# One PSUM bank pair per gate, shared by both halves of a column, in the recurrent layer of a two-layer kernel

## The chip, the cores and the metric

The kernel runs on one core of one Trainium2 chip. The core has TensorE (PE, matrix products), VectorE (DVE), ScalarE (ACT), GpSimd (POOL) and SyncE (SP, which issues DMAs). Each engine takes its own instructions in order, and they wait for each other through semaphores. Matrix products are written to PSUM, here eight banks of 512 fp32 values for each of 128 partitions. The metric is the time of one execution on the device in microseconds (us), lower is better.

## The reference

The input x has shape (4, 64, 256, 256) in fp32. Two layers follow, each added to its input:

```
x = x + L0(groupnorm(x))      # patchwise FFT attention; the change does not touch it
x = x + L1(groupnorm(x))      # below

f = transpose(features, (3, 0, 2, 1))          # columns first: W, B, H, C
def step(prev_col, cur_col):                   # once per column, 255 times
    x = concat([prev one row up, prev, prev one row down])       # 3 x 64 channels
    gi = x @ w_ih.T + b_ih
    gh = cur_col @ w_hh.T + b_hh
    r = sigmoid(i_r + h_r)
    z = sigmoid(i_z + h_z)
    n = tanh(i_n + r * h_n)
    return (1 - z) * n + z * cur_col
```

So layer 1 is a recurrent cell that runs over the 256 columns one after the other. A row of a new column needs three rows of the column before it (itself and its two neighbours).

## The kernel before

**Layer 0** takes the first 4368 us or so. Nothing in it changes.

**Layer 1** (from line 683 to the end of the kernel function) goes through the columns in the loop `for w in range(W)`. The 128 partitions hold two images' 64 channels, and a second index of size 2 (`slot`) the other two, so one instruction works on all four images. A weight is 64 by 64, so a product over all images is four "quarter" matmuls, one for each pair (r, c) of the list `QUARTERS`: r is the half of the partitions that is read, c the half that is written. The four run in different quarters of the array. Each fp32 matmul shows in the trace as two records and two weight loads.

A column's 256 rows are cut in two parts so that one part's matmuls can run while the other's gates are worked out. `parts(w)` gives the cut. It starts at row 144, is one row less in each next column, down to 113, and after 32 columns jumps back to 144. Because it moves by a row a column, part 0 needs only part 0 of the column before. Only where the cut jumps back (columns 33, 65, 97, 129, 161, 193, 225) does part 0 also need part 1 of the column before.

`begin(w, part)` (line 753) does one part; it is called at lines 820 and 821. On PE, in this order, each item being four quarter matmuls:

- h_n (weights `wh[:, 2]` times the column itself) into tile `hr`, index 0
- h_r (`wh[:, 0]`) and three taps of i_r (`wi[:, 0..2]` times the state of the column before, moved by 0, 1 and 2 rows) into `hr`, index 1
- three taps of i_n into tile `nz`, index 0
- h_z and three taps of i_z into `nz`, index 1

Then on ACT and DVE: sigmoid of r (`g`, ACT), a normalisation for a column eight ahead (`xn`, ACT), (h_n + bias) times r (`n`, DVE), plus i_n (`n`, DVE), tanh (`n`, ACT), sigmoid of z (`z`, ACT), and three DVE instructions that end in the new state (`st`). Per column that is ten DVE instructions and eight ACT instructions, part 0's before part 1's on each engine.

The instructions stand on each engine in the order in which the program issues them; the class `InOrder` sees to that. The framework puts in the waits. A PSUM tile of a given tag that is asked for again waits until the last reader of the earlier one is done.

PSUM: the tags are `hr0`, `nz0`, `hr1`, `nz1`, one for each part, and each is two banks, one for each half r. One bank holds two gates side by side (index 0 and 1), 256 values each. That makes 4 x 2 = 8 banks, all there are.

The trace puts every operation on line 156, that of the helper that records the order, so the tiles' names tell the operations apart.

Of the kernel before, what the change touches and what calls it, by code (L numbers as in the profile page):

```python
# [10 lines left out]
F32 = mybir.dt.float32  # L11
AF = mybir.ActivationFunctionType
ALU = mybir.AluOpType
# [3 lines left out]
B, C, W, H = 4, 64, 256, 256  # L17
HID = 6 * C
E = 2 * C
P = 128  # L20
# [141 lines left out]
def tile_conv_then_gru(  # L162
# [17 lines left out]
    nc = InOrder(tc, tc.nc)  # L180
# [25 lines left out]
    wi = const.tile([P, 9, C], F32, tag="wi", name="wi")  # L206
    wh = const.tile([P, 3, C], F32, tag="wh", name="wh")
    for a in range(2):
        at = slice(a * C, (a + 1) * C)
# [3 lines left out]
    bias_sb = const.tile([P, 6], F32, tag="bias", name="bias_sb")  # L213
    nc.scalar.dma_start(bias_sb, bias.rearrange("a o n -> (a o) n"))
    b_rz = const.tile([P, 2], F32, tag="b_rz", name="b_rz")
# [5 lines left out]
    with tc.tile_pool(name="xa", bufs=3) as xa, tc.tile_pool(name="sta", bufs=1) as sta, tc.tile_pool(  # L221
        name="gnps", bufs=1, space=PSUM
# [6 lines left out]
        for kind in range(2):  # L229
            bt = sta.tile([9, NS, HALO], F32, tag="bt", name=f"bt_{kind}")  # L230
            nc.scalar.dma_start(bt, taps[:, kind * NS : (kind + 1) * NS, :])
            for s in range(0, NS, 4):
                to = ts[0:2] if kind == 0 else ts[2:3]
                ps = bps.tile([HALO, 4, len(to) * P], F32, tag="b", name=f"psb_{kind}_{s}")
                for i in range(4):
                    nc.tensor.matmul(
                        ps[:, i, :],
                        lhsT=bt[:, s + i, :],
                        rhs=wd[:, 0 : 2 * P] if kind == 0 else wd[:, 2 * P : 3 * P],
                        start=True,  # L240
                        stop=True,
# [11 lines left out]
        for j in range(NPAIR):  # L253
            st = sta.tile([P, NST, 6], F32, tag="st", name=f"st_{j}", bufs=2)
# [9 lines left out]
        for b in range(B):  # L264
            at = slice((b % 2) * C, (b % 2) * C + C)
# [8 lines left out]
    with ExitStack() as s:  # L274
# [18 lines left out]
        z = big.tile([P, NP, NS], F32, tag="z", name="z")  # L293
# [389 lines left out]
    WB = 8  # L683
    with ExitStack() as s:
        rawp = s.enter_context(tc.tile_pool(name="raw", bufs=3))
        colp = s.enter_context(tc.tile_pool(name="cols", bufs=2))
        gk = s.enter_context(tc.tile_pool(name="gk", bufs=2))
        ps_g = s.enter_context(tc.tile_pool(name="ps_g", bufs=1, space=PSUM))
        raws, xns, xts, stcols = {}, {}, {}, {}

        def columns(m, w):

            yield m[:, :, w, :].rearrange("(k a) c h -> (a c) k h", k=NPAIR), slice(0, P), 0
            for half in range(2):
                b0 = SLOTS[1][0][half]
                yield m[b0 : b0 + 2, :, w + 1, :].rearrange("b c h -> c b h"), slice(half * C, half * C + C), 1

        def load_columns(w):
            n, i = w // WB, w % WB
            if i == 0:  # L700
                raws[n] = rawp.tile([P, 2, WB, H], F32, tag="raw", name=f"raw_{n}")
            for of, at, j in columns(x1, w):
                nc.sync.dma_start(raws[n][at, :, i + j], of)

        def new_columns(n):
            xns[n] = colp.tile([P, 2, WB, H], F32, tag="xn", name=f"xn_{n}")
            xts[n] = colp.tile([P, WB, H], F32, tag="xt", name=f"xt_{n}")

        def empty_states(n):
            stcols[n] = st = colp.tile([P, 2, WB, H + 2], F32, tag="st", name=f"st_{n}")  # L710
            nc.gpsimd.memset(st[:, :, :, 0:1], 0.0)
            nc.gpsimd.memset(st[:, :, :, H + 1 : H + 2], 0.0)

        def normalize(w, slot):
            n, i = w // WB, w % WB
            if i == slot == 0:
                new_columns(n)
            nc.scalar.activation(
                xns[n][:, slot, i],
                raws[n][:, slot, i],  # L720
                AF.Identity,
                bias=sc1[:, w % 2, slot, 0:1],
                scale=sc1[:, w % 2, slot, 1:2],
            )
            if slot and i % 2:

                for half in range(2):
                    nc.sync.dma_start(
                        xts[n][half * C : (half + 1) * C, i - 1 : i + 1],
                        xns[n][(1 - half) * C : (2 - half) * C, half, i - 1 : i + 1],  # L730
                    )

        def add(w):
            n, i = w // WB, w % WB
            nc.gpsimd.tensor_tensor(
                raws[n][:, :, i], raws[n][:, :, i], stcols[n][:, :, i, 1 : H + 1], ALU.add
            )
            if i % 2:
                for of, at, j in columns(out, w - 1):
                    nc.sync.dma_start(of, raws[n][at, :, i - 1 + j])  # L740

        QUARTERS = ((0, 0), (0, 1), (1, 0), (1, 1))
        SKEW = 32

        def parts(w):


            at = H // 2 + SKEW // 2 - (w - 1) % SKEW
            return (0, at), (at, H)

        MAX = H // 2 + SKEW // 2

        def begin(w, part):

            h0, h1 = parts(w)[part]
            i, num = w % WB, h1 - h0
            xn, xt, st = xns[w // WB], xts[w // WB], stcols[w // WB]
            before = stcols[(w - 1) // WB]
            prev = before[:, :, (w - 1) % WB, h0 : h1 + 2]

            cur = {
                (r, c): (xn[:, c] if r == c else xt)[r * C : (r + 1) * C, i, h0:h1] for r, c in QUARTERS
            }
            prevs = [
                {(r, c): prev[r * C : (r + 1) * C, c, t : t + num] for r, c in QUARTERS} for t in range(3)
            ]

            hr = ps_g.tile([P, 2, 2, H], F32, tag=f"hr{part}", name=f"pshr_{w}_{part}")
            nz = ps_g.tile([P, 2, 2, H], F32, tag=f"nz{part}", name=f"psnz_{w}_{part}")

            def quarters(ps, k, weights, rhs, start, stop):
                for r, c in QUARTERS:
                    at = slice(r * C, (r + 1) * C)
                    nc.tensor.matmul(
                        ps[c * C : (c + 1) * C, r, k, 0:num],
                        lhsT=weights[at],
                        rhs=rhs[r, c],
                        start=start,
                        stop=stop,
                        tile_position=(r * C, c * C),  # L780
                    )

            quarters(hr, 0, wh[:, 2, :], cur, True, True)
            quarters(hr, 1, wh[:, 0, :], cur, True, False)
            for t in range(3):
                quarters(hr, 1, wi[:, t, :], prevs[t], False, t == 2)
            for t in range(3):
                quarters(nz, 0, wi[:, 6 + t, :], prevs[t], t == 0, t == 2)
            quarters(nz, 1, wh[:, 1, :], cur, True, False)
            for t in range(3):  # L790
                quarters(nz, 1, wi[:, 3 + t, :], prevs[t], False, t == 2)
            g = gk.tile([P, 2, MAX], F32, tag=f"g{part}", name=f"g_{w}_{part}")[:, :, 0:num]
            n = gk.tile([P, 2, MAX], F32, tag=f"n{part}", name=f"n_{w}_{part}")[:, :, 0:num]
            z = gk.tile([P, 2, MAX], F32, tag=f"z{part}", name=f"z_{w}_{part}")[:, :, 0:num]
            nc.scalar.activation(g, hr[:, :, 1, 0:num], AF.Sigmoid, bias=b_rz[:, 0:1], scale=1.0)
            if w + WB < W:
                normalize(w + WB, part)
            nc.vector.scalar_tensor_tensor(
                n, hr[:, :, 0, 0:num], bias_sb[:, 5:6], g, ALU.add, ALU.mult
            )  # L800
            nc.vector.tensor_tensor(n, nz[:, :, 0, 0:num], n, ALU.add)
            nc.scalar.activation(n, n, AF.Tanh, bias=bias_sb[:, 2:3], scale=1.0)
            nc.scalar.activation(z, nz[:, :, 1, 0:num], AF.Sigmoid, bias=b_rz[:, 1:2], scale=1.0)
            nc.vector.tensor_tensor(g, xn[:, :, i, h0:h1], n, ALU.subtract)
            nc.vector.tensor_tensor(g, g, z, ALU.mult)
            nc.vector.tensor_tensor(st[:, :, i, 1 + h0 : 1 + h1], g, n, ALU.add)

        for w in range(0, 2 * WB, 2):
            load_columns(w)
        for w in range(WB + 1):  # L810
            for slot in range(2):
                normalize(w, slot)
        empty_states(0)
        nc.vector.tensor_copy(stcols[0][:, :, 0, 1 : H + 1], xns[0][:, :, 0])
        for w in range(W):
            n, i = w // WB, w % WB
            if i == 0 and n + 1 < W // WB:
                empty_states(n + 1)
            if w:
                begin(w, 0)  # L820
                begin(w, 1)
            add(w)
            if i % 2 and w + 2 * WB < W:
                load_columns(w + 2 * WB - 1)
# [55 lines left out]
```

## Time and profile before

| | |
|---|---|
| time, median of 3 runs | 5980.89 us (5962.14 to 5995.17) |
| the profiled execution, its own time | 5966.15 us |
| its span, first to last instruction | 5964.4 us |
| mean granted TensorE clock | 0.994 |
| PE busy | 5552.3 us, 93% of the span |
| DVE busy | 4085.5 us, 68% |
| ACT busy | 3438.4 us, 58% |
| POOL busy | 398.9 us, 7% |
| first and last `n` of layer 1 on DVE start at | 4400.6 and 5954.8 us |

Busy time is the time in which at least one instruction of the engine runs. Matmuls are pipelined and the ends of their records are modelled, so a busy PE is not a PE at its limit. "x24" in a line means that so many records follow each other. A form such as 128x284 counts partitions by elements: 284 is a part of 142 rows for both slots. In brackets stands how long the engine was idle before an instruction and what released it; "issue" is idle time in which the engine waited for nothing that the profile shows. Layer 1's matmuls are those that write `pshr` and `psnz`; those that write `psring` are layer 0's.

### The profile page before, as it was taken

The page shows a single profiled execution, that of the slowest core. Times are in us where ns is not written, and L with a number is a line of the kernel's source. Part 1 is how long each engine was busy: PE and PEld are TensorE (multiplying, and loading weights), DVE is VectorE, ACT ScalarE, POOL GpSimd, SP SyncE. Part 2 cuts the span into 40 slices and gives each one's busy share as a digit, 9 for nine tenths or more (in the row PEclk, how much of TensorE's full clock was granted, in tenths as well). Part 3 has the DMA queues.
Part 4 walks back from the last instruction along what each step waited for, and adds up shares of the span by engine and source line. Part 5 has one row for each costly group of instructions (what it writes and reads, how often), then busy time and mean ns, then how long its engine had stood idle before and what let it go on. Part 6 is the DMA issues. An engine that isn't in the chain of part 4 may idle for free.

```text
span 5964.4 us, 282969 instructions
## 1 busy us (share of the span) xinstructions
PE 5552.3 (93%) x129224; PEld 4814.1 (81%) x129224; DVE 4085.5 (68%) x9549; ACT 3438.4 (58%) x4617; POOL 398.9 (7%) x602
## 2 busy tenths in 40 slices
PE   5499999999999999999999999999979999999998
PEld 4388888888887888887888888888868888888888
DVE  7567776666776667677666767667666666666666
ACT  1266656566665656665656666565645555555554
POOL 0000000000000000000000000000002111122121
PEclk9999999999999999999999999999989999999999
DMA  9545454444444444545444544544444444444442
GB/s 386 210 133 151 132 138 143 125 140 145 137 134 138 127 138 142 145 125 146 134 134 131 150 133 131 145 125 141 123 123 111 112 111 110 110 112 113 110 112 80
DMA packets 549714, 818.06 MB, mean 137 GB/s; under 512 B 38443, under 2 KB 432436, under 8 KB 544404
## 3 DMA queue, kind: packets, MB, share of 16 engines
q1 hardware_dynamic: 523264, 683.80, 40.6%
q0 software_dynamic: 22320, 114.70, 5.8%
q8 instruction: 1012, 16.58, 1.2%
q10 hardware_dynamic: 2934, 1.46, 0.1%
q14 instruction: 184, 1.51, 0.1%
HBM read 622.22 MB, written 144.05 MB: 128 GB/s over the span
## 4 chain that ended last, share of the span: by engine, by line
PE 52%; DVE 14%; ACT 6%; issue 4%; DMA 2%; SPq 0%; DVEq 0%; ACTq 0%; POOLq 0%
PE psring L156 45%; DVE g L156 5%; DVE n L156 5%; PE psnz L156 4%; ACT n L156 3%; PE pshr L156 3%; DVE st L156 3%; DMA t<-t_all 2%; ACT v L156 1%; ACT z L156 1%; ACT h L156 0%; DVE z L156 0%; SPq L156 0%; DVEq L156 0%; ACTq L156 0%
## 5 line engine op out<-in xcount | busy, mean ns | idle before, releaser
L156 PEld LDWEIGHTS psring<-h,t 100*32 100x32 f32 x40960 | 1335.6, 115 | 267.1 <-issue 184.3
L156 PE MATMUL psring<-h,t 100*32 100x128 f32 x40960 | 1438.8, 274 | 86.6 <-ACT h L156 35.6
L156 PEld LDWEIGHTS psring<-w_sb,xq 64*100 64x100 f32 x24576 | 1350.2, 163 | 83.0 <-issue 43.6
L156 PE MATMUL psring<-w_sb,xq 64*100 64x128 f32 x24576 | 1391.3, 270 | 25.0 <-POOL xq L156 19.9
L156 ACT COPY h<-psring 100x1024 f32<-100x1024 f32 x1274 | 1203.0, 1027 | 142.4 <-PE psring L156 136.4
L156 PE MATMUL psnz<-st,wi 64*64 64x115 f32 (+16 forms) x24480 | 919.3, 271 | 24.9 <-issue 24.0
L156 PEld LDWEIGHTS psnz<-st,wi 64*64 64x64 f32 x24480 | 778.4, 133 | 46.2 <-issue 45.1
L156 DVE TENSOR_TENSOR pr<-psring,q 128x512 f32<-128x512 f32 (+1 forms) x576 | 464.0, 861 | 339.5 <-PE psring L156 335.8
L156 ACT ACTIVATE n<-n,bias_sb 128x288 f32<-128x288 f32 (+7 forms) x510 | 259.8, 509 | 665.0 <-DVE n L156 665.0
L156 DVE BATCH_NORM_STATS2 lnst<-z 128x6 f32<-128x64 f32 x4096 | 545.2, 214 | 118.2 <-ACT z L156 118.2
L156 DVE TENSOR_TENSOR z<-z,lnm 128x1024 f32<-128x1024 f32 x512 | 612.7, 1218 | 8.7
L156 ACT COPY q<-psring 128x1024 f32<-128x1024 f32 x256 | 259.1, 1012 | 522.4 <-PE psring L156 456.9
L156 PE MATMUL pshr<-st,wi 64*64 64x144 f32 (+7 forms) x12240 | 478.1, 275 | 79.2 <-DVE st L156 63.9
L156 ACT COPY z<-psring 128x2048 f32<-128x2048 f32 x128 | 238.8, 1866 | 499.3 <-PE psring L156 499.3
L156 PE MATMUL psring<-pr,g_sb 32*64 32x512 f32 x8192 | 488.7, 599 | 8.3 <-issue 8.3
L156 ACT ACTIVATE y<-psring,ln_sb 128x512 f32<-128x512 f32 x512 | 372.1, 781 | 200.8 <-PE psring L156 196.9
L156 PEld LDWEIGHTS pshr<-st,wi 64*64 64x64 f32 x12240 | 363.8, 133 | 149.3 <-DVE st L156 93.7
L156 DVE COPY h<-psring 100x1024 f32<-100x1024 f32 x262 | 320.4, 1223 | 217.5 <-PE psring L156 215.3
L156 DVE TENSOR_TENSOR g<-xn,n 128x288 f32<-128x288 f32 (+7 forms) x510 | 217.4, 426 | 325.2 <-ACT n L156 325.2
L156 DVE TENSOR_TENSOR y<-psring,y 128x1024 f32<-128x1024 f32 x256 | 312.3, 1220 | 118.3 <-ACT y L156 116.8
L156 POOL TENSOR_TENSOR raw<-raw,st 128x512 f32<-128x512 f32 x256 | 303.4, 1185 | 1234.0 <-DVE st L156 652.2
L156 PE MATMUL pshr<-xn,wh 64*64 64x144 f32 (+7 forms) x4080 | 354.4, 270 | 9.6 <-ACT xn L156 6.5
(88 smaller groups left out, 6368.5 us busy)
## 6 DMA issues: line engine op xcount, KB each, us to landing
t<-t_all SPq DMA_DIRECT2D x768, 400.0 KB
xq<-in_xh POOLq DMA_DIRECT2D x128, 800.0 KB, 4.6
xc<-in_x SPq DMA_DIRECT2D x32, 2048.0 KB
xr<-in_x SPq DMA_DIRECT2D x256, 256.0 KB
x<-xr SPq DMA_DIRECT2D x256, 256.0 KB
raw<-x SPq DMA_DIRECT2D x128, 256.0 KB
raw<-x SPq DMA_DIRECT2D x256, 128.0 KB
xt<-xn SPq DMA_DIRECT2D x256, 128.0 KB
```

The costliest lines, as they stand in the source:

```text
L156: return self.tc.keep_in_program_order(got(*args, **kwargs))
```

## The change

`begin` becomes `column(w)`, which issues the matmuls of both parts, and `state(w, part, ...)`, which issues a part's ACT and DVE work. Each gate now has a bank pair of its own (tags `hn`, `hr`, `ni`, `hz`, again 4 x 2 = 8 banks), and for `hr`, `ni` and `hz` the two parts take it in turn. h_n is computed once a column over all 256 rows, one matmul per quarter, before everything else of the column; the parts read their rows of it. The arithmetic is the same, and ACT's and DVE's instructions stand in the same order. The order of PE's work in a column is now h_n; h_r and i_r, i_n, h_z and i_z of part 0; the same of part 1. That is 92 matmuls a column where there were 96.

```diff
-        def begin(w, part):
+        def bank_pair(gate, w):
+            return ps_g.tile([P, 2, 512], F32, tag=gate, name=f"ps{gate}_{w}")
+
+        def quarters(ps, weights, rhs, start, stop):
+            for r, c in QUARTERS:
+                nc.tensor.matmul(
+                    ps[c * C : (c + 1) * C, r],
+                    lhsT=weights[r * C : (r + 1) * C],
+                    rhs=rhs(r, c),
...
+        def column(w):
+
+            i, xn, xt, st = w % WB, xns[w // WB], xts[w // WB], stcols[(w - 1) // WB]
+
+            def own(ps, gate, h0, h1, stop):
...
+            def taps(ps, gate, h0, h1, start):
+                for t in range(3):
...
+            pn = bank_pair("hn", w)[:, :, 0:H]
+            own(pn, 2, 0, H, True)
+            for part in range(2):
+                h0, h1 = parts(w)[part]
+                pr, pi, pz = (bank_pair(gate, f"{w}_{part}")[:, :, 0 : h1 - h0] for gate in ("hr", "ni", "hz"))
+                own(pr, 0, h0, h1, False)
+                taps(pr, 0, h0, h1, False)
+                taps(pi, 2, h0, h1, True)
+                own(pz, 1, h0, h1, False)
+                taps(pz, 1, h0, h1, False)
+                state(w, part, pn[:, :, h0:h1], pr, pi, pz)
+
+        def state(w, part, pn, pr, pi, pz):
...
-            hr = ps_g.tile([P, 2, 2, H], F32, tag=f"hr{part}", name=f"pshr_{w}_{part}")
-            nz = ps_g.tile([P, 2, 2, H], F32, tag=f"nz{part}", name=f"psnz_{w}_{part}")
...
-            quarters(hr, 0, wh[:, 2, :], cur, True, True)
-            quarters(hr, 1, wh[:, 0, :], cur, True, False)
-            for t in range(3):
-                quarters(hr, 1, wi[:, t, :], prevs[t], False, t == 2)
-            for t in range(3):
-                quarters(nz, 0, wi[:, 6 + t, :], prevs[t], t == 0, t == 2)
-            quarters(nz, 1, wh[:, 1, :], cur, True, False)
-            for t in range(3):
-                quarters(nz, 1, wi[:, 3 + t, :], prevs[t], False, t == 2)
...
-            nc.scalar.activation(g, hr[:, :, 1, 0:num], AF.Sigmoid, bias=b_rz[:, 0:1], scale=1.0)
+            nc.scalar.activation(g, pr, AF.Sigmoid, bias=b_rz[:, 0:1], scale=1.0)
...
-            nc.vector.scalar_tensor_tensor(
-                n, hr[:, :, 0, 0:num], bias_sb[:, 5:6], g, ALU.add, ALU.mult
-            )
-            nc.vector.tensor_tensor(n, nz[:, :, 0, 0:num], n, ALU.add)
+            nc.vector.scalar_tensor_tensor(n, pn, bias_sb[:, 5:6], g, ALU.add, ALU.mult)
+            nc.vector.tensor_tensor(n, pi, n, ALU.add)
...
-            nc.scalar.activation(z, nz[:, :, 1, 0:num], AF.Sigmoid, bias=b_rz[:, 1:2], scale=1.0)
+            nc.scalar.activation(z, pz, AF.Sigmoid, bias=b_rz[:, 1:2], scale=1.0)
...
             if w:
-                begin(w, 0)
-                begin(w, 1)
+                column(w)
```

More of the change, by code (lines that the diff above doesn't have):

```diff
@@ L751, in tile_conv_then_gru @@
         MAX = H // 2 + SKEW // 2
-        def begin(w, part):
+        def bank_pair(gate, w):
[6 more added lines that the diff above has]
+                    rhs=rhs(r, c),
+                    start=start,
+                    stop=stop,
+                    tile_position=(r * C, c * C),
+                )
@@ new lines, in column @@
+        def column(w):
+            i, xn, xt, st = w % WB, xns[w // WB], xts[w // WB], stcols[(w - 1) // WB]
+            def own(ps, gate, h0, h1, stop):
+                quarters(
+                    ps,
+                    wh[:, gate, :],
+                    lambda r, c: (xn[:, c] if r == c else xt)[r * C : (r + 1) * C, i, h0:h1],
+                    True,
+                    stop,
+                )
+            def taps(ps, gate, h0, h1, start):
+                for t in range(3):
+                    quarters(
+                        ps,
+                        wi[:, 3 * gate + t, :],
+                        lambda r, c: st[r * C : (r + 1) * C, c, (w - 1) % WB, h0 + t : h1 + t],
+                        start and t == 0,
+                        t == 2,
+                    )
+            pn = bank_pair("hn", w)[:, :, 0:H]
[9 more added lines that the diff above has]
+                state(w, part, pn[:, :, h0:h1], pr, pi, pz)
@@ L755, in begin @@
+        def state(w, part, pn, pr, pi, pz):
             h0, h1 = parts(w)[part]
             i, num = w % WB, h1 - h0
[L757 to L766, printed above, removed]
@@ L768, in begin @@
-            hr = ps_g.tile([P, 2, 2, H], F32, tag=f"hr{part}", name=f"pshr_{w}_{part}")
-            nz = ps_g.tile([P, 2, 2, H], F32, tag=f"nz{part}", name=f"psnz_{w}_{part}")
[L771 to L780, printed above, removed]
-                    )
@@ L783, in begin @@
-            quarters(hr, 0, wh[:, 2, :], cur, True, True)
-            quarters(hr, 1, wh[:, 0, :], cur, True, False)
-            for t in range(3):
-                quarters(hr, 1, wi[:, t, :], prevs[t], False, t == 2)
-            for t in range(3):
-                quarters(nz, 0, wi[:, 6 + t, :], prevs[t], t == 0, t == 2)
-            quarters(nz, 1, wh[:, 1, :], cur, True, False)
-            for t in range(3):
-                quarters(nz, 1, wi[:, 3 + t, :], prevs[t], False, t == 2)
+            xn, st = xns[w // WB], stcols[w // WB]
@@ L794, in begin @@
             z = gk.tile([P, 2, MAX], F32, tag=f"z{part}", name=f"z_{w}_{part}")[:, :, 0:num]
-            nc.scalar.activation(g, hr[:, :, 1, 0:num], AF.Sigmoid, bias=b_rz[:, 0:1], scale=1.0)
+            nc.scalar.activation(g, pr, AF.Sigmoid, bias=b_rz[:, 0:1], scale=1.0)
             if w + WB < W:
                 normalize(w + WB, part)
-            nc.vector.scalar_tensor_tensor(
-                n, hr[:, :, 0, 0:num], bias_sb[:, 5:6], g, ALU.add, ALU.mult
-            )
-            nc.vector.tensor_tensor(n, nz[:, :, 0, 0:num], n, ALU.add)
+            nc.vector.scalar_tensor_tensor(n, pn, bias_sb[:, 5:6], g, ALU.add, ALU.mult)
+            nc.vector.tensor_tensor(n, pi, n, ALU.add)
             nc.scalar.activation(n, n, AF.Tanh, bias=bias_sb[:, 2:3], scale=1.0)
-            nc.scalar.activation(z, nz[:, :, 1, 0:num], AF.Sigmoid, bias=b_rz[:, 1:2], scale=1.0)
+            nc.scalar.activation(z, pz, AF.Sigmoid, bias=b_rz[:, 1:2], scale=1.0)
             nc.vector.tensor_tensor(g, xn[:, :, i, h0:h1], n, ALU.subtract)
```

## The prediction

> **What bounds the kernel now.** The page's chain of waits gives most of the span to TensorE in the first layer ("PE psring L156 45%"), which the change doesn't touch. So I left the page and read layer 1 alone, from about 4400 us to the end. First the busy time by stretch (columns: stretch, its length, then busy us and count for PE, weight loads, DVE, ACT, POOL; then clock, DMA share, GB/s):
>
> ```profile
> 5200.00:5400.00 200.00, 184.66 (x6316) 172.52 (x6312) 137.86 (x329) 112.95 (x263) 39.70 (x41) 1.00 0.41 112
> ```
>
> PE looks full (92%) and DVE not (69%). The timeline of DVE says otherwise. One column, in order (start, length, instruction, idle time before it and its releaser):
>
> ```profile
> 5199.99 0.51 DVE L156 SCALAR_TENSOR_TENSOR n<-pshr,bias_sb,g 128x284 f32<-128x284 f32 x1
> 5200.60 0.46 DVE L156 TENSOR_TENSOR n<-psnz,n 128x284 f32<-128x284 f32 x1
> 5201.71 0.46 DVE L156 TENSOR_TENSOR g<-xn,n 128x284 f32<-128x284 f32 x1 [0.66 <-ACT n L156]
> ...
> 5203.14 0.45 DVE L156 SCALAR_TENSOR_TENSOR n<-pshr,bias_sb,g 128x228 f32<-128x228 f32 x1
> ...
> 5205.95 0.51 DVE L156 SCALAR_TENSOR_TENSOR n<-pshr,bias_sb,g 128x282 f32<-128x282 f32 x1
> ```
>
> From one column's first DVE instruction to the next column's: 5.96 us. In it DVE runs ten instructions back to back and stops twice, each time for its own tanh on ACT (0.66 and 0.61 us). It never waits for PE. The chain of waits over 5190 to 5230 confirms it:
>
> ```profile
> by line: DVE g L156 29.6%; DVE n L156 27.2%; ACT n L156 15.6%; DVE st L156 14.9%; issue 9.6%; DVEq L156 1.4%; ACT z L156 1.1%; ACT g L156 1.0%; ACTq L156 0.6%
> ```
>
> No PE in it. PE waits for the state instead, 0.48 us in this column. The DVE list is the same before and after the change, so 5.96 us a column is a floor that the change can't move. Waits of layer 1 (total us, times, longest):
>
> ```profile
> DVE g L156 <- ACT n L156: 324.5, 509, 0.9
> ...
> PE pshr L156 <- DVE st L156: 63.9, 136, 3.0
> ...
> DVE n L156 <- ACT g L156: 33.6, 8, 20.5
> ...
> DVE n L156 <- PE psnz L156: 24.0, 47, 2.3
> ```
>
> The last two rows are what PE costs DVE: 20.5 of the 33.6 is the start of the layer, the rest the seven columns where the boundary jumps back; 24.0 is DVE waiting for the bank of n and z.
>
> **How much lies above the floor.** By the tile answers, n's first DVE instruction starts at 4400.6 and the last (part 1 of column 255) at 5954.8. Less 3.15 for part 0 to part 1 in a column, 254 columns took 1551.0 us. 254 x 5.96 is 1513.8. So 37.2 us are above the floor, in three kinds.
>
> *Boundary columns* (seven: part 0 needs part 1 of the column before). An undisturbed one:
>
> ```profile
> 5769.74 0.97 PE L156 MATMUL pshr<-st,wi 64*64 64x144 f32 x24 [2.96 <-DVE st L156]
> 5770.50 0.94 PE L156 MATMUL psnz<-st,wi 64*64 64x144 f32 x24
> ...
> 5771.30 0.52 DVE L156 SCALAR_TENSOR_TENSOR n<-pshr,bias_sb,g 128x288 f32<-128x288 f32 x1 [1.71 <-ACT g L156]
> ...
> 5771.48 0.94 PE L156 MATMUL psnz<-st,wi 64*64 64x144 f32 x24
> ...
> 5772.48 0.46 DVE L156 TENSOR_TENSOR n<-psnz,n 128x288 f32<-128x288 f32 x1 [0.66 <-PE psnz L156]
> ```
>
> The addition of i_n starts at 5772.48, just after the z matmuls end (5771.48 + 0.94 = 5772.42), although the i_n matmuls end a microsecond earlier: n and z share a bank pair. Two columns take 14.34 us here (5763.48 to 5777.82), 2.42 over the floor; seven times, 16.9 us.
>
> *Half clock.* In four of the seven, PE's clock record shows 0.5 for 3.4 us after the long idle stretch, and the same matmuls take nearly twice as long (1.68 where it was 0.94):
>
> ```profile
> 4790.99 0.99 PE L156 MATMUL pshr<-st,wi 64*64 64x144 f32 x24 [2.96 <-DVE st L156]
> 4791.75 1.68 PE L156 MATMUL psnz<-st,wi 64*64 64x144 f32 x24
> ```
>
> These four cost 6.4 us more (three by 1.66, one by 1.43).
>
> *Hiccups*, the other 13.9 us. PE stops for "issue" every 128 matmul records:
>
> ```profile
> 4621.38 0.47 PE L156 MATMUL psnz<-st,wi 64*64 64x140 f32 x8 [0.46 <-issue]
> ...
> 4625.40 0.70 PE L156 MATMUL pshr<-st,wi 64*64 64x139 f32 x16 [0.36 <-issue]
> ...
> 4629.42 0.43 PE L156 MATMUL psnz<-st,wi 64*64 64x117 f32 x8 [0.25 <-issue]
> ```
>
> They are 4.02 us apart. The DMA view counts 382 instruction packets (6.26 MB, 16 KB each) for PE's 382 blocks of 256 instructions (a matmul record and its weight load each count one).
>
> **What the Trainium skill says.** "PSUM — Partial Sum Buffer", section "PSUM bank collisions raise a hardware error", tells to guard by bank, not by address: two engines may not touch one bank and quadrant at once. That is why the addition waits for z (0.66 us above; agrees). "TensorE: Matmul & The Clock Gate", Part 1: a window of about 3.4 us with too little PE work halves the clock; the four half-clock stretches agree. "Runtime: NRT & Kernel Launch", section "Instruction fetch mechanics": refill in 16 KiB blocks of 256 instructions, "mostly hidden"; the block size agrees, the hiding fails here.
>
> **The change part by part.** One group of four quarter matmuls (eight records) costs 1.70 ns a column of its width: 24 records of 141 columns take 0.72 us (5204.05 to 5204.77).
>
> 1. *h_n in one matmul per quarter.* Same streamed width, 256 instead of 144 + 112, so no PE time; four matmuls fewer a column: 16 of 384 PE instructions, 4.2%. The width 256 isn't in the trace before; from the rate, 256 x 1.70 = 0.44 us. The nearest wider row (8192 records of 512 columns, 488.7 us busy, eight to a round) gives 0.48 for 512 in one pass, so 0.24 for 256 and 0.48 for the two passes. I take 0.44; bounds 0.40 to 0.88 (no overlap of quarters).
>
> 2. *i_n in a bank of its own.* In the boundary columns the addition no longer waits for z. i_n ends at 5771.23 + 0.24; the product before it ends at 5771.82; the addition starts at 5771.92, 0.56 earlier. Seven times: **-3.9 us**. Elsewhere the wait was hidden already: nothing.
>
> 3. *One bank pair per gate for both parts: new waits.* Part 1's r waits for part 0's sigmoid, its i_n for part 0's addition, its z for part 0's z sigmoid. In the column above, PE would come to part 1's r after the sigmoid of part 0 (4.90 + 0.49 = 5205.39), to i_n about 0.5 us after the addition ends (5207.02), to z about when the sigmoid ends; each is due on ACT or DVE only later. Nothing.
>
> 4. *h_n waits for part 1 of the column before.* This is the wait that matters: one h_n pair, freed by part 1's first DVE instruction, and behind it on PE, which takes matmuls in order, stands all of the next column. DVE frees it at 5203.14 + 0.45 = 5203.59 and wants the next sigmoid for 5205.95: 2.36 us. The way through: hand-over 0.06 (state end to matmul, above), h_n 0.44, r's own 0.24, taps 0.72, end of the last 0.245 (0.97 less 0.72), 0.06, sigmoid 0.49, 0.03: 2.28. Margin 0.08. With part 0 at 143: 2.33 against 2.29, margin 0.04. With part 0 at 113 (5760.84 to 5763.48): 2.64 against 2.04, margin 0.60. So it just fits: nothing, but the cover is thin, 0.32 on average, where r had over a microsecond.
>
> 5. *Half clock.* In a boundary column h_n now can't start before 5766.86 + 0.06, so PE's idle 2.96 us splits into about 0.6 before h_n and 2.1 after r's own. The shorter stretches should halve the clock about twice in place of four times: **-3 us** (0 to -6).
>
> 6. *Hiccups.* At 4.02 us a block, 384 instructions take 6.03 us a column, over the floor; 368 take 5.78, under it. Most should be hidden; those that hit h_n or r (22% of the stream) have less cover than before. I take half of the 13.9: **-8 us** rounded, bounds +5 to -13.
>
> No DMA, ACT or POOL instruction moves. Sum: -3.9 - 3 - 8 = **-15 us**. The profiled execution took 5966.15 us (span 5964.4 and 1.75 around it), so 5951; the median shown, 5980.89, is 14.7 above it, so **5966** on that scale. A measurement here tells no change from about 0.5%, 30 us: this forecast is "within".
>
> **Rivals.**
> - *Nothing comes of it* (0 us, 5981): hiccups now strike the thin chain of step 4 and give back what steps 2 and 5 bring. For it: 0.04 of margin at the start of each 32 columns. Against: fewer instructions.
> - *All of it comes* (5942): all removable excess goes, 37.2 less 7 x 1.86 that the boundary needs, 24 us, and the 15 us by which the median exceeds the profiled run were hiccups of layer 1 too. Against: the first layer, 70% of the time and full of PE, can hold those 15.
> - *Slower, the h_n bank is the new loop* (6021): if h_n with its hand-over costs 0.5 us more than I say (quarters that hardly overlap), step 4's chain passes DVE's wherever the margin is less. Margins are spread evenly from 0.04 to 0.60, so the mean loss is 0.46 squared / (2 x 0.56) = 0.19 us on 247 columns, 47 us, less 7 from steps 2 and 5: +40. It decides from about 0.1 us, and passes 0.5% near 0.45. Against: 512-wide matmuls overlap well in the first layer.
>
> **Numbers.** Forecast 58%, nothing 20%, all 13%, slower 9%. Forecast's own range 5948 to 5985. Taking in half of the outer cases and the spread of the runs (5962 to 5995): 5940 to 5992. Faster by over 0.5%: 0.17 (all of it, and a little of the forecast); slower 0.09; within 0.74.
>
> **What would show it.** Right: DVE's column still 5.96 us; boundary columns some 0.56 shorter, the row "DVE n <- PE" nearly gone; PE waiting at pshn for DVE n in most columns, 0.5 to 0.9 us; fewer "issue" stops. Wrong: "DVE n <- ACT g" in ordinary columns (step 4 lost), above all just after a boundary column; or a DVE column below 5.96, which would mean that I misread the floor.

## The result and the profile after

The changed kernel takes 5958.19 us in the median (5941.98 to 5977.76, 20 runs) against 5979.01 us before, 20.8 us less. The ratio is 0.9966 with a 95% interval of 0.9957 to 0.9976: a gain of a third of a percent, clear of noise. The forecast was 5966 us and "within 0.5%". On a second chip the ratio came out as 0.9912 (0.9894 to 0.9929), a gain of 49.7 us; see experiment 6.

In the profiled executions the span goes from 5964.4 to 5950.2 us, 14.2 less. "Layer 1" below means the time from the first column's first DVE instruction to the last column's: 1551.3 us before, 1533.7 after, 17.6 less. The part ahead of it, where nothing was changed, took 3.5 us longer this time.

DVE's waits in layer 1 after the change (total us, times, longest):

```profile
DVE g L156 <- ACT n L156: 325.2, 510, 1.0
DVE n L156 <- ACT g L156: 34.2, 8, 21.2
...
DVE n L156 <- PE pshz L156: 0.9, 2, 0.5
DVE n L156 <- PE psni L156: 0.8, 2, 0.4
```

The two tanh waits of each column are where they were. The row with PE's `psnz`, 24.0 us in 47 waits before, has shrunk to 1.7 us in four.

A boundary column in the timeline after (start, length, engine, instruction, idle before it):

```profile
4789.08 0.97 PE L156 MATMUL pshr<-st,wi 64*64 64x144 f32 x24 [1.92 <-DVE st L156]
4789.84 0.94 PE L156 MATMUL psni<-st,wi 64*64 64x144 f32 x24
4790.64 0.52 DVE L156 SCALAR_TENSOR_TENSOR n<-pshn,bias_sb,g 128x288 f32<-128x288 f32 x1 [1.71 <-ACT g L156]
4790.82 0.94 PE L156 MATMUL pshz<-st,wi 64*64 64x144 f32 x24
4791.26 0.46 DVE L156 TENSOR_TENSOR n<-psni,n 128x288 f32<-128x288 f32 x1
```

The addition starts at 4791.26 while the z matmuls still run to 4791.76. Before, it waited for their end. The pair of columns around an undisturbed jump takes 13.78 us in place of 14.34 (7.82 + 5.96 against 7.82 + 6.52).

An ordinary column, again from the timeline after:

```profile
5203.96 0.45 DVE L156 SCALAR_TENSOR_TENSOR n<-pshn,bias_sb,g 128x232 f32<-128x232 f32 x1
...
5204.47 0.43 PE L156 MATMUL pshn<-xn,wh 64*64 64x256 f32 x1 [0.49 <-DVE n L156]
...
5205.19 0.89 PE L156 MATMUL pshr<-st,wi 64*64 64x139 f32 x24
...
5206.15 0.49 ACT L156 ACTIVATE g<-pshr,b_rz 128x278 f32<-128x278 f32 x1 [0.30 <-PE pshr L156]
...
5206.79 0.50 DVE L156 SCALAR_TENSOR_TENSOR n<-pshn,bias_sb,g 128x278 f32<-128x278 f32 x1
```

This is the new chain of step 4. Part 1's first DVE instruction ends at 5204.41 and frees the h_n bank, PE starts h_n at 5204.47, and the sigmoid that hangs on it ends at 5206.64. DVE, which comes round for it at 5206.79, is not held up, by 0.15 us. The chain of waits over 5210 to 5250 shows how close the two chains have come. Before there was no PE in it:

```profile
by line: DVE n L156 24.3%; DVE g L156 21.8%; ACT n L156 14.3%; DVE st L156 10.7%; issue 9.2%; PE pshr L156 6.8%; PE pshz L156 4.4%; PE psni L156 3.9%; PE pshn L156 2.7%; ACT g L156 1.2%; DVEq L156 1.2%; ACTq L156 0.5%
```

Where the 17.6 us went, from the start times of the columns, always over a floor of 5.957 us a column: the 14 columns around the seven jumps lie 15.6 us over the floor (23.4 before), the other 240, called ordinary below, 5.0 us (14.9 before). PE stops for issue are down from 107 to 29 in these two executions, and the half-clock stretches from four to two. A stop is counted here and below when it is over 0.06 us; the waits view lists those over 0.15 us.

### The profile page after: what moved, and what is told of

It reads as the page before. It is cut to its first block, busy times and chain, and to the rows that moved or that the text cites. A ratio compares the mean times of both kernels' runs of the same rounds, so it can differ in the third digit from the quotient of the medians.

```text
span 5950.2 us, 278865 instructions
## 1 busy us (share of the span) xinstructions
PE 5537.8 (93%) x127184; PEld 4770.7 (80%) x127184; DVE 4085.5 (69%) x9549; ACT 3465.8 (58%) x4617; POOL 399.5 (7%) x602
## 4 chain that ended last, share of the span: by engine, by line
PE 64%; DVE 18%; ACT 7%; DMA 5%; issue 5%; SPq 0%; DVEq 0%; ACTq 0%; POOL 0%; POOLq 0%
PE psring L156 61%; DVE g L156 7%; DVE n L156 6%; DVE st L156 4%; ACT n L156 4%; DMA t<-t_all 2%; DMA xc<-in_x 2%; ACT v L156 2%; ACT z L156 1%; PE pshr L156 1%; PE pshz L156 1%; PE psni L156 1%; ACT h L156 1%; PE pshn L156 0%; SPq L156 0%
## 5 line engine op out<-in xcount | busy, mean ns | idle before, releaser
L156 PE MATMUL psring<-w_sb,xq 64*100 64x128 f32 x24576 | 1394.2, 271 | 27.3 <-POOL xq L156 17.8
L156 PE MATMUL pshr<-st,wi 64*64 64x144 f32 (+7 forms) x12240 | 433.3, 270 | 14.0 <-DVE st L156 13.4
L156 PE MATMUL psni<-st,wi 64*64 64x144 f32 (+7 forms) x12240 | 438.4, 270 | 8.0 <-issue 6.6
L156 PE MATMUL pshz<-st,wi 64*64 64x144 f32 (+7 forms) x12240 | 436.6, 269 | 1.8 <-issue 1.1
L156 PEld LDWEIGHTS psni<-st,wi 64*64 64x64 f32 x12240 | 361.5, 133 | 13.5 <-issue 9.9
```

Of the source, the lines that this page charges most:

```text
L156: return self.tc.keep_in_program_order(got(*args, **kwargs))
```

## The experiments

Two theories of the gain stood against each other. One: PE's stops are rarer because PE has fewer instructions (step 6 of the prediction). The other: the banks do it, because a stop hurts only where DVE waits for PE. Under both lies a claim that is tested first, that DVE with its two tanh waits is the floor.

**1. z without its taps.** In the changed kernel a quarter of PE's work is left out: z is the sigmoid of h_z and the bias alone.

```diff
-                own(pz, 1, h0, h1, False)
-                taps(pz, 1, h0, h1, False)
+                own(pz, 1, h0, h1, True)
```

> The changed kernel without the three taps of i_z (24 of 92 matmuls a column are left out; z is then the sigmoid of h_z and the bias alone). PE has 1.3 us less to do a column. Theory (DVE with its two tanh waits sets 5.96 us a column): layer 1 loses only what is left of PE stops and half clock, so 1526 to 1533 us, time 5950 to 5958. Rival (PE, 92 percent busy, is the bound): 254 x 1.3 us less, about 330 us, time near 5630.

Measured: 5958.82 us, ratio 0.997 (0.996 to 0.9979); layer 1 1534.9 us. Busy time by stretch of this kernel (PE, weight loads, DVE, ACT, POOL, clock, DMA share, GB/s):

```profile
5200.00:5360.00 160.00, 124.85 (x3588) 99.75 (x3592) 110.91 (x264) 93.50 (x212) 31.36 (x32) 1.00 0.41 112
```

PE is down from some 92% to 78%, and the time hasn't moved. PE's work is not what sets the column. The last few us that I expected didn't come either: this trace has no PE stop at all, but half clock at four of the seven jumps. Its ordinary columns still lie 5.7 us over the floor, so the 5.0 us that the changed kernel has left there need no PE stops to explain them.

**2. Two DVE instructions less a column.** The other side of the same question: the last addition is left out of both parts, so the new state is (x - n) times z.

```diff
-            nc.vector.tensor_tensor(g, g, z, ALU.mult)
-            nc.vector.tensor_tensor(st[:, :, i, 1 + h0 : 1 + h1], g, n, ALU.add)
+            nc.vector.tensor_tensor(st[:, :, i, 1 + h0 : 1 + h1], g, z, ALU.mult)
```

> The changed kernel with the last addition left out: the new state is (x - n) times z, so each part has four DVE instructions in place of five. Theory (DVE's list with its tanh waits sets the column): the floor falls by about 0.9 us to 5.04; then PE (5.22 us of matmuls) and the chain of the h_n bank (2.28 + 3.60 - 0.49 = 5.39 at 141 rows, 4.99 at 113) take over, some 5.3 us a column, layer 1 near 1365 us, time 5770 to 5800. Rival (PE is the bound already): at most 10 us off 5958.

Measured on the second chip: ratio 0.9848 (0.9811 to 0.9884), 5911.83 us; layer 1 1479.0 us. The direction is as expected and the size is not: columns at their best take 5.23 to 5.39 us, as worked out, but their mean is 5.82. DVE now waits for the sigmoid of r about once a column, where it did so eight times in the changed kernel, so the chain of the h_n bank has taken over, as expected:

```profile
DVE n L156 <- ACT g L156: 157.5, 265, 20.3
```

What holds this chain back further is in PE's waits:

```profile
PE psni L156 <- issue: 27.9, 46, 1.6
PE pshz L156 <- issue: 24.7, 48, 1.2
PE pshr L156 <- issue: 23.2, 35, 1.8
```

PE stops 163 times for 81 us. The DMA view of layer 1 counts the blocks in which PE's instructions arrive:

```profile
q8 instruction: 364, 5.96, 1.7%
```

Every one of the 163 stops ends between 1.2 and 1.8 us after such a block has landed, with blocks some 4 us apart, so what PE waits for is its instructions. The 95 ordinary columns without a stop take 5.43 us on average, the 145 with one 6.04. That difference goes with the stops. It is not shown to be a fixed rate of the blocks: 364 blocks in 1479 us are one every 4.06 us, and 1.44 blocks a column (368 instructions) times 4.06 give 5.82 us, but that is the mean column over again and no second measurement of it; 28 columns in a row took only 5.68 each.

**3. h_n issued twice.** The margin of step 4, measured by using it up.

```diff
             own(pn, 2, 0, H, True)
+            own(pn, 2, 0, H, True)
```

> The changed kernel with the four h_n matmuls of a column issued twice (the second overwrites the first, same values): +0.44 us of PE behind the wait for part 1's first DVE instruction. Theory (the way from there to the next column's sigmoid has a margin of 0.04 us at part 0 = 143 rows rising to 0.60 at 113): columns of large part 0 take up to 0.40 us more, those below about 121 rows take 5.96 as before, mean 0.14 us, layer 1 +35 us, time 5985 to 6000. Rival (the margin is wide, since PE idles 0.5 us or more before h_n in most columns): within 5 us of 5958. Rival (no margin at all): +0.44 in every column, +110 us.

Measured: 5988.25 us, ratio 1.0022 (1.0011 to 1.0033); layer 1 1566.3 us, 32.6 more than the changed kernel. DVE in the column after a jump now waits for the sigmoid:

```profile
5795.85 0.39 DVE L156 TENSOR_TENSOR st<-g,n 128x224 f32<-128x224 f32 x1
5796.54 0.52 DVE L156 SCALAR_TENSOR_TENSOR n<-pshn,bias_sb,g 128x286 f32<-128x286 f32 x1 [0.30 <-ACT g L156]
```

Row by row, for columns of the last stretch of 32 that nothing else disturbed (margin and excess in us; the margin on a straight line from 0.04 at 143 rows to 0.60 at 113):

| rows of part 0 | margin, predicted | 0.44 less margin | column over 5.957, measured |
|---|---|---|---|
| 143 | 0.04 | 0.40 | 0.37 |
| 134 | 0.21 | 0.23 | 0.21 |
| 131 | 0.26 | 0.18 | 0.15 |
| 128 | 0.32 | 0.12 | 0.09 |
| 125 | 0.38 | 0.06 | 0.05 |
| 122 | 0.43 | 0.01 | 0.00 |

The h_n bank is a chain with just the margin that the trace before gave, some 0.03 us more.

**4. i_n and z in one bank pair again**, all else as changed.

```diff
-                pr, pi, pz = (bank_pair(gate, f"{w}_{part}")[:, :, 0 : h1 - h0] for gate in ("hr", "ni", "hz"))
+                pr = bank_pair("hr", f"{w}_{part}")[:, :, 0 : h1 - h0]
+                nz = ps_g.tile([P, 2, 2, H], F32, tag=f"nz{part}", name=f"psnz_{w}_{part}")
+                pi, pz = (nz[:, :, k, 0 : h1 - h0] for k in range(2))
```

> The changed kernel with i_n and z again side by side in one bank pair per part, h_n and r as changed, order of the matmuls as changed. Theory: only the columns at a jump of the cut notice; in each the addition of i_n waits 0.66 us for the z matmuls again and a pair of columns takes 14.34 in place of 13.78 us, so layer 1 rises by 3.9 us, time about 5962; PE stops for issue as few as after the change. Rival (the own bank of i_n is what hides PE's stops in all columns): many ordinary columns show DVE waiting for PE again, layer 1 rises by 10 us or more, time 5968 or above.

Measured: 6013.99 us, ratio 1.0059 (1.0046 to 1.0072), slower than the kernel before. The theory's 3.9 us came nowhere near. The rival's "10 us or more" takes in the 56 us, but lost cover for PE's stops can't be all of it: the kernel before has the shared bank and the stops too, and is faster. A new theory was worked out for the next trace.

> The same kernel as in the run before with i_n and z in one bank pair, for an undisturbed profile: its time was 6014 us, 56 above the changed kernel, where 3.9 was expected. New theory: with h_n ahead of r in one shared pair the matmuls of part 0 start after part 1's first DVE instruction, about 1 us later than before the change, so the z matmuls of part 0 end after the moment at which DVE wants i_n: by the rates of the trace 0.47 us late at 143 rows, nothing at 113. Columns should grow from 5.96 at small part 0 to about 6.5 at large, layer 1 about 1580 to 1590 us, DVE's waits for PE in the addition some 40 to 55 us in total, nearly all in columns with part 0 above 125 rows. Rival (some other wait, of z or of r): the waits stand elsewhere or in all columns alike.

Measured (one run on the second chip): layer 1 1589.5 us; DVE's row for PE in the addition:

```profile
DVE n L156 <- PE psnz L156: 74.8, 174, 1.9
```

Undisturbed columns lie 0.52 us over the floor at 143 rows, 0.27 at 134, 0.11 at 128 and 0.00 at 122. In the first of these, from DVE's timeline and PE's:

```profile
5838.07 0.51 DVE L156 SCALAR_TENSOR_TENSOR n<-pshn,bias_sb,g 128x286 f32<-128x286 f32 x1
5839.20 0.46 DVE L156 TENSOR_TENSOR n<-psnz,n 128x286 f32<-128x286 f32 x1 [0.62 <-PE psnz L156]
```

```profile
5838.22 0.91 PE L156 MATMUL psnz<-st,wi 64*64 64x143 f32 x24
```

These z matmuls end at 5839.13, and the addition that needs only i_n starts at 5839.20. The new theory holds; the total of the waits, 75 us, is above my 40 to 55, which left out the jumps and PE's stops (44 here). The shared h_n bank makes PE late by about as much as the own bank of i_n lets it be, and without that bank the change makes the kernel slower. The other half alone, an own bank for i_n with h_n as before, was not run. Where i_n and z share a bank pair they are also one tile of the program, in this kernel and in the one before, so whether the wait goes by the bank, as the prediction says, or by the tile stays open.

**5. h_n in two matmuls per quarter again**, 384 PE instructions, new banks.

```diff
-            own(pn, 2, 0, H, True)
+            for h0, h1 in parts(w):
+                own(pn[:, :, h0:h1], 2, h0, h1, True)
```

> The changed kernel with h_n again in two matmuls per quarter (rows of part 0, rows of part 1) into the same shared bank pair, at the same place: 96 matmuls a column, 384 PE instructions, banks as changed. Layer 1 means from the first column's to the last column's first DVE instruction: 1551.3 us before, 1533.7 after. Theory (PE's instruction blocks arrive at about 4.02 us each; 368 instructions a column hide them, 384 do not): the columns at a jump stay 0.56 us shorter than before, but PE stops for issue come back as often as before (about 107 against 29) and layer 1 rises by 6 to 12 us, time about 5966. Rival A (the banks alone made the gain): stops stay near 29 and the time at 5958. Rival B (the thin margin of the h_n chain loses more to such stops than the old order did): slower than before, above 5979.

Measured: 5962.91 us, ratio 0.9974 (0.9965 to 0.9983), which can't be told from the changed kernel's. PE's stops are back, 101 of them for 37 us, but layer 1 takes 1534.9 us, 1.2 more than the changed kernel. Two differences lie in the 1.2: the ordinary columns are 8.5 us over the floor, 3.5 more than the changed kernel's, and the jumps 13.3, 2.3 less, as no jump met half clock in this trace. Nor does the number of PE instructions alone decide how often PE stops: experiment 3's kernel has 384 a column too, and its trace has seven stops.

**6. The old kernel with 92 matmuls.** The converse: old banks, old order, part 1's h_n left out, with the sum for r read in its place.

```diff
-            quarters(hr, 0, wh[:, 2, :], cur, True, True)
+            if part == 0:
+                quarters(hr, 0, wh[:, 2, :], cur, True, True)
...
-                n, hr[:, :, 0, 0:num], bias_sb[:, 5:6], g, ALU.add, ALU.mult
+                n, hr[:, :, part, 0:num], bias_sb[:, 5:6], g, ALU.add, ALU.mult
```

> The kernel before with part 1's h_n matmuls left out (part 1's product reads the sum for r in their place): old banks, old order, but 92 matmuls and 368 PE instructions a column as after the change, and 0.2 us less of PE. Theory (fewer PE instructions hide the arrival of PE's instruction blocks): PE stops for issue fall from 107 to about 30; the columns at a jump still take 14.34 us a pair; layer 1 falls from 1551 by 4 to 10 us, ratio to before 0.998 to 0.9993. Rival (the stops have another cause than the number of instructions): about 107 stops, ratio 1.

Measured on the second chip: 109 stops, no fewer than the old kernel's 107 on the first; layer 1 1550.0 us. By stops and layer 1 the theory fails, if traces of two chips may be set against each other (the ordinary columns lie 3.7 us lower, the jumps 2.3 higher, with half clock at six of them). By the times of one chip it does not: the ratio is 0.9947 (0.9928 to 0.9965), as this kernel took 5982.93 us where the kernel before took 6014.84. Beside it ran the changed kernel:

> The changed kernel itself, beside the next one on the same chip: ratio to before 0.9966 as measured, layer 1 1530 to 1536 us.

Measured: 5965.13 us, ratio 0.9912 (0.9894 to 0.9929); layer 1 1537.0 us with 61 stops. The kernel before had no trace on that chip. The next two were meant to give one, and to repeat the fifth experiment there:

> The kernel before itself, for a trace on the chip on which it took 6015 us where the kernel with 92 matmuls and the old banks took 5983 with a layer 1 of 1550.0 us and 109 PE stops for issue. Theory (the number of PE instructions matters through the stops): layer 1 is 25 to 40 us longer than 1550, with more or longer stops, and the part ahead of layer 1 is the same. Rival (the 32 us come from the part ahead of layer 1, where the kernels are the same but for where their instructions lie): layer 1 near 1551 and the first instruction of layer 1 on DVE 25 to 40 us later than the 4413 of that run.

> The changed kernel with h_n in two matmuls per quarter again (384 PE instructions, new banks) on the same chip. Theory (banks and number of instructions both count): layer 1 between the changed kernel's 1537 and the old one's, stops over 100, ratio 0.993 to 0.998. Rival (only the banks count): 1537 and 0.991. Rival (only the number counts): layer 1 and ratio as of the kernel before.

Both came to the first chip instead, where the kernel before took 5994.62 us this time (5977.54 beside experiments 1 and 3 to 5), so that times are to be compared within one series only. The kernel before (1.0004 of itself, 0.9991 to 1.0016): layer 1 1561.9 us, 186 stops. The two-matmul kernel: ratio 0.9959 (0.9946 to 0.9972), layer 1 1546.7 us, 182 stops. DVE's waits tell what such stops do. The kernel before, second trace:

```profile
DVE n L156 <- PE psnz L156: 39.7, 92, 2.2
DVE n L156 <- ACT g L156: 34.2, 8, 21.5
```

New banks with two matmuls, second trace:

```profile
DVE n L156 <- ACT g L156: 39.0, 27, 21.1
DVE g L156 <- ACT z L156: 2.4, 7, 0.9
...
DVE n L156 <- PE pshz L156: 0.9, 2, 0.5
...
DVE n L156 <- PE psni L156: 0.4, 1, 0.4
```

In the next table the last two columns are us over the floor, as in the section on the result. Where there are two values, the second trace of the changed kernel is from the second chip, the other second traces are from the first.

| kernel | PE stops | layer 1, us | ordinary columns | columns at the jumps |
|---|---|---|---|---|
| before | 107, 186 | 1551.3, 1561.9 | 14.9, 26.3 | 23.4, 22.6 |
| before with 92 matmuls (second chip) | 109 | 1550.0 | 11.2 | 25.7 |
| changed, h_n in two matmuls | 101, 182 | 1534.9, 1546.7 | 8.5, 19.2 | 13.3, 14.4 |
| changed | 29, 61 | 1533.7, 1537.0 | 5.0, 7.4 | 15.6, 16.5 |

With about as many stops, the new banks save 15 to 16 us (1551.3 to 1534.9, 1561.9 to 1546.7). In the ordinary columns they save 6.4 and 7.1 us; the rest stands at the jumps, where part of it is half clock that came less often. From there to the changed kernel the ordinary columns come down by another 3.5 us in sum (first traces), with 101 stops down to 29. In its first trace the stops cost nothing any more: the 28 ordinary columns with a stop take 5.98 us on average, as do the other 212, where the kernel before takes 6.08 with and 5.99 without. So both theories have a share in the traces of the first chip, the banks the larger one.

What the four matmuls are worth apart from the banks isn't settled. By the times of the first chip the two-matmul kernel (0.9974 and 0.9959) equals the changed one (0.9966). By those of the second chip the old banks with 92 matmuls save 31.9 us of the 49.7, and the new banks the other 17.8. The kernel before was never traced there, so where it loses the 31.9 us is open. The number of stops differs by a factor of nearly two between executions of one kernel, and each of these comparisons rests on one trace a side.

**7. A version beyond both.** If a column is ten DVE instructions and two waits, another part's work can fill the waits. Same instructions, other order:

```
PE   h_n, r 0, i_n 0, r 1, z 0, i_n 1, z 1
ACT  g 0, xn, tanh 0, g 1, z 0, tanh 1, xn, z 1
DVE  n 0, +i_n 0, x-n 0, n 1, +i_n 1, *z 0, st 0, x-n 1, *z 1, st 1
```

> The changed kernel with the same instructions in another order: on PE h_n, r 0, i_n 0, r 1, z 0, i_n 1, z 1; on DVE part 1's first two instructions stand between part 0's subtraction and its product with z, on ACT the sigmoid of r 1 right behind the tanh of part 0. Nothing is left out. Theory (a column is DVE's ten instructions, 4.7 us, and two tanh waits of 0.6 that another part's work can fill): worked through with the durations of the trace a column takes about 5.6 us on average, jumps included, in place of 6.04, so layer 1 about 1440 us and time 5850 to 5890. Rival (PE is the bound): no gain, since PE has the same matmuls. Rival (the banks taken in turn turn the new order into waits of PE): slower than 5958.

> The kernel with the parts interleaved again, on the same chip as the changed one: ratio to before 0.986 to 0.991, so 0.8 percent below the changed kernel; undisturbed columns at 5.62 to 5.70 us, layer 1 1495 to 1515 us.

Measured: ratio 0.9883 (0.9856 to 0.9909), then 0.9875 (0.9852 to 0.9899) beside the changed kernel's 0.9912: 5938.80 against 5965.13 us, and layer 1 1504 against 1537. An undisturbed column, DVE's timeline:

```profile
4695.87 0.48 DVE L156 SCALAR_TENSOR_TENSOR n<-pshn,bias_sb,g 128x256 f32<-128x256 f32 x1
...
4697.89 0.48 DVE L156 SCALAR_TENSOR_TENSOR n<-pshn,bias_sb,g 128x256 f32<-128x256 f32 x1
4698.60 0.42 DVE L156 TENSOR_TENSOR n<-psni,n 128x256 f32<-128x256 f32 x1 [0.23 <-PE psni L156]
...
4700.51 0.43 DVE L156 TENSOR_TENSOR g<-g,z 128x256 f32<-128x256 f32 x1 [0.36 <-ACT z L156]
...
4701.50 0.48 DVE L156 SCALAR_TENSOR_TENSOR n<-pshn,bias_sb,g 128x254 f32<-128x254 f32 x1
```

5.63 us, as worked out: the tanh wait of part 1 is gone and two shorter ones have come. But the mean column takes 5.92 us and layer 1 1504 to 1506, not the 1440 expected. This order has little slack left for PE's stops, which I had left out of that sum: in the second trace the 180 ordinary columns without a stop take 5.72 us on average, the 60 with one 6.38.

## Why the prediction was right

*The floor* (5.96 us a column, DVE and two tanh waits) held: ordinary columns after are at 5.957 in the median. Less PE work changed nothing, less DVE work did. The stretch that was taken as 1551.0 us is 1551.3, as the two parts of the last column start 2.81 us apart and not 3.15.

*Step 1* said 0.44 us for the wide h_n: after, h_n starts at 5204.47 and the next group at 5204.95, 0.48.

*Step 2*, -3.9 us at the jumps: undisturbed pairs are 0.56 shorter, seven times 3.9. That it brings nothing elsewhere, as the wait "was hidden already", was wrong: with as many PE stops the new banks take 6.4 and 7.1 us off the ordinary columns (experiment 6), and once h_n's wait makes PE late, the own bank is worth 0.5 us a column at 143 rows (experiment 4).

*Step 3*, the banks taken in turn at nothing: right; in layer 1 after the change PE waits at z for ACT twice, 0.3 and 0.2 us, and once at i_n for DVE, 0.8 us (waits over 0.15 us).

*Step 4*, the margin of 0.04 to 0.60: right to 0.03 us (experiment 3). The slower rival was therefore real, with the point from which it decides where it was put: twice h_n made the kernel slower than before.

*Step 5*, half clock from four to two jumps: two in the first trace after. Over all traces with the old banks (three) it came at 13 of 21 jumps, with the new banks and full work on PE (changed twice, two matmuls twice, h_n issued twice once) at 6 of 35. In the other traces of experiments it came at four of seven with less PE work (1), four of seven with i_n and z together (4), and none of 21 with the columns shorter (2 and 7). "TensorE: Matmul & The Clock Gate", Part 1, names a window of about 3.4 us with too little work; PE's idle stretch at a jump is down from 2.96 to 1.92 us, and the stretches at half clock last 3.4 us here. That agrees; at which of the jumps, whose idle stretches are alike, the clock halves is not explained.

*Step 6*, hiccups, is right in size and only in part in its reason. It took half of 13.9 us, -8; the ordinary columns gave -9.9, all that PE's stops could be blamed for, as about 5 us stay even with none (experiment 1). But it gave the whole to the number of instructions, 368 fitting the rate of the blocks where 384 don't. PE stopped at 107 of 381 blocks before, not at every one, and 4.02 us is no fixed rate: with 384 instructions the ordinary columns have a median of 5.96 us, before and in experiment 5, which is a block every 3.97. What the runs put in its place: 6.4 us of it come with the banks at 384 instructions, because a stop in front of or among the z matmuls no longer reaches the addition (DVE's waits for PE there fall from 92 to three in the second traces), and 3.5 us go with fewer stops. That 16 instructions fewer are what makes the stops rarer isn't shown: 384 gave 7 to 186 of them, 368 gave 29 to 163. The cover that I feared to be thinner was thicker for i_n and thinner for r only: DVE's waits for the sigmoid of r are up from 8 to 27 in those traces.

In sum -3.9, -3 and -8 were forecast, 15 us; the traces gave 7.8 at the jumps and 9.9 elsewhere, and 3.5 of loss ahead of layer 1 that is no part of the change, together the 14.2 us of the spans. That the sum comes so close is luck in part: "half" was a guess, and the medians differ by 20.8. On the second chip the gain is 49.7 us, three times the forecast and no longer "within 0.5%"; why, stays open.

## What to carry to other kernels

Before pricing a change on the busiest engine, follow one period of the loop on every engine: here PE was 92% busy and its work bound nothing, while DVE at 69% waited in an ordinary column only for its own chain. When buffers are given out anew, write down for each the last reader that frees it and the time until its next user is due; that margin, row by row, told what the change could bear. Two accumulations that shared a tile and its banks were one to the instruction that waited for the first, and it showed only when the second was late. And a rate worked out from a total and a count is the mean period over again; whether it limits anything is read from the single stops.

## What the runs showed of the hardware

PE can stop for want of instructions, and the stops can be told from other idle time: all 163 in experiment 2 end 1.2 to 1.8 us after the landing of a block of 256 instructions. There an ordinary column with a stop takes 0.6 us longer than one without (6.04 against 5.43); in the changed kernel's first trace, with 29 stops, no longer at all. "Runtime: NRT & Kernel Launch", section "Instruction fetch mechanics", has the 16 KiB block and calls its cost mostly hidden; in experiments 2 and 7 it is not. What decides how often PE stops, these runs don't show.
